# Summing the exponentials of both key halves on TensorE in a conditioned transformer block

## The chip, the cores and the metric

The kernel runs on one core of one Trainium2 chip. The metric is the time of one execution on the device in microseconds; lower is better. Before the change it is 2498.34 us, the median of three runs (2495.81 to 2498.56).

## The reference

One pre-norm transformer block in fp32 on `x` of 4 x 1024 x 512, with norms whose gain and bias come from a conditioning vector. There are 16 heads of 32 channels and 2048 hidden channels.

```python
g = t @ gw.T + gb; b = t @ bw.T + bb
norm(x) = g * x * rsqrt(mean(x * x) + EPS) + b
attn = (q . k) / sqrt(32); p = softmax(attn); o = (p . v)
x1  = x  + o @ Wo.T
x2  = x1 + (silu(n @ gate_w.T) * (n @ hid_w.T)) @ out_w.T    # n = norm2(x1)
out = x + x2
```

What matters here is the softmax: every query needs the sum of its exponentials over all 1024 keys, for each head.

## The kernel before, in words

Activations lie channels first: partitions are channels, columns are tokens. Attention works on units `j`: one batch element and half a block of 512 queries (so 256 queries, `HQ`), and one group of four heads (`HG`). There are 64 units. A unit takes its 1024 keys in four steps `r` (`UN` = 4) of two key tiles of 128 keys each. A step's scores are one tile `raw[r]` of 128 partitions (keys) by 2 x 4 x 256 columns: key tile `k` in 0..1, head, query.

A step passes through these operations, named as in the code:

- `scores` (TensorE, L301) computes the scores, `keep` (ScalarE, L308) copies them out of PSUM, and `running_max` (VectorE, L313 and L316) keeps the largest per head and query over the keys that share a partition.
- After the four steps, `max_T` (TensorE, L322), `parts` (VectorE, L328 to L333), `parts_T` (L338, L340) and `spread` (L348, L349) turn the maximum into a tile `shift` that every key's partition can add.
- `shifted` (VectorE, L354) adds it, `exponential` (ScalarE, L357) takes the exponential in place, and `weighted` (TensorE, L367) multiplies with the values into `av`.
- `accumulate` (L381) adds the step's exponentials onto those of the unit's first step. This is a DMA that adds, issued by GpSimd, over all 2 x 4 x 256 columns. So after four steps the tile `acc[j]` holds, for each partition, key tile `k`, head and query, the sum over four steps.
- `fold_sum` (VectorE, L389) then adds the half `k` = 1 onto the half `k` = 0, 128 x 1024 numbers.
- `sums` (TensorE, L399) sums over the partitions: one matmul with a 128 x 32 tile of ones for each head, so that the head's 32 output partitions all hold the sum. `sums_out` (ScalarE, L404), `inverse` (L407) and `normalize` (L416) follow.

The order on TensorE, VectorE, ScalarE and GpSimd is written out by hand in one loop over `g`, one step of scores in each turn; each engine works through its own list in that order. `kind` is `g % 4`. Behind the scores of step `g` come `shifted` and `exponential` of step `g - 5` and `weighted` of step `g - 6`. `fold_sum` of a unit stands at the end of the turn of kind 3, and `sums` of the same unit in the next turn, of kind 0, ahead of `max_T` of a later unit. The last DMA of `accumulate` was issued two turns before `fold_sum`.

The rest of the work fills the same turns. In the first 500 us these are the projections (`project_kq`, `project_v`) and norms of later batch elements; from about 540 us it is the feed-forward part, one hidden tile of 128 channels in two turns. Its seven products for a tile (a Strassen-like scheme) go by `pair_15`, `pair_26`, `pair_7`, `pair_3` and `pair_4` into the PSUM tiles `pa` and `pb`; around them stand `take_5` (L511) and `copy_156` (L530) on ScalarE, `add_15` (L515) and `sub_5` (L537) on VectorE, `gate` (L552) and `hidden` (L555). `contract` (tile `pc`) multiplies four hidden tiles with the output weights, and `take_contract` (L568) adds that onto the result. `add_15` stands on VectorE just ahead of `fold_sum`, `hidden` just behind it. In some turns `token_sums` (L482 to L488), `norm_squares` (L132 to L138), `norm_root` (tiles `pma` and `pmf`) and `project_out` (tile `po`) come in too. After 2213 us no attention unit is left, only the last output projection, its norm and the feed-forward part.

`sum`, `pc`, `pa`, `pt`, `sp`, `pma` and others share two PSUM banks (tag `w`, two buffers): a matmul into a new tile waits until the tile two before it has been read out.

Of the kernel before, what the change touches and what calls it, by code (L numbers as in the profile page):

```python
# [13 lines left out]
ALU = mybir.AluOpType  # L14
# [10 lines left out]
def tile_cond_transformer_block(  # L25
# [13 lines left out]
    nc = tc.nc  # L39
# [7 lines left out]
    DH = D // N_HEADS  # L47
    HG = P // DH
# [22 lines left out]
    ones_sum = const.tile([P, DH], F32, tag="ones_sum", name="ones_sum")  # L71
# [39 lines left out]
    raw, rmax, shift, mT, av, acc, avs, oT = {}, {}, {}, {}, {}, {}, {}, {}  # L111
# [180 lines left out]
    def scores(r: int):  # L292

        j, u = divmod(r, UN)
        m, qh = divmod(j, NB // HQ)
        keys, queries = kq[m, 0, u], kq[m, 1, qh]
        sc = ps_sc.tile([P, HG, 2, HQ], F32, tag="sc", name=f"sc{r}")
        for k in range(2):
            for i in range(HG):
                rows = slice(i * DH, (i + 1) * DH)  # L300
                nc.tensor.matmul(  # L301
                    sc[:, i, k, :], keys[rows, k * P : (k + 1) * P], queries[rows, :], start=True, stop=True
                )
        state["sc", r] = sc
# [30 lines left out]
    def parts_T(j: int):  # L335
        pt = ps.tile([P, HQ // P, P], BF16, tag="w", name=f"pt{j}")
        for qt in range(HQ // P):
            nc.tensor.transpose(pt[:, qt, :], split[j % 2][:, qt, :], ident_bf)  # L338
        mT[j] = sb.tile([NP, HQ], BF16, tag="mT", name=f"mT{j}", bufs=2)
        nc.scalar.copy(mT[j], pt[:NP, :, :].rearrange("p a b -> p (a b)"))  # L340

    def spread(j: int, k: int):

        if k == 0:
            shift[j] = sb.tile([P, HG, HQ], F32, tag="shift", name=f"shift{j}")
        pp = ps.tile([P, 2, HQ], F32, tag="w", name=f"sp{j}_{k}")
        for i in range(2):
            nc.tensor.matmul(pp[:, i, :], select[:, k + i, :], mT[j], start=True, stop=True)  # L348
        nc.scalar.copy(shift[j][:, k : k + 2, :], pp)  # L349
# [6 lines left out]
    def exponential(r: int):  # L356
        nc.scalar.activation(raw[r], raw[r], AF.Exp)  # L357
# [26 lines left out]
                accum_op=ALU.add,  # L384
            )

    def fold_sum(j: int):
        t = acc[j]
        nc.vector.tensor_tensor(t[:, 0, :, :], t[:, 0, :, :], t[:, 1, :, :], ALU.add)  # L389

    def take_av(j: int):
        avs[j] = sb.tile([P, HQ], F32, tag="avs", name=f"avs{j}", bufs=2)
        nc.scalar.copy(avs[j], av.pop(j))

    def sums(j: int):
        total = ps.tile([P, HQ], F32, tag="w", name=f"sum{j}")
        a = acc.pop(j)
        for i in range(HG):
            nc.tensor.matmul(total[i * DH : (i + 1) * DH, :], ones_sum, a[:, 0, i, :], start=True, stop=True)  # L399
        state["sum", j] = total  # L400

    def sums_out(j: int):
# [3 lines left out]
    def inverse(j: int):  # L406
        nc.vector.reciprocal(state["total", j], state["total", j])  # L407
# [280 lines left out]
    with tc.manual_schedule(  # L688
# [69 lines left out]
        while g < END:  # L758
            kind = g % UN
            r_x, r_v = g - UN - 1, g - UN - 2  # L760
            x_on, v_on = 0 <= r_x < NR, 0 <= r_v < NR
            j_m = g // UN - 1
            m_on = 0 <= j_m < NR // UN
            j_s = g // UN - 2
            s_on = 0 <= j_s < NR // UN
            j_n = g // UN - 3
            n_on = 0 <= j_n < NR // UN
            ffn = g >= FS
            p = (g - FS) // 2
            even = g % 2 == 0  # L770
            columns[0] = DH

            if kind == 1 and m_on:
                parts_T(j_m)
            if g < NR:
                scores(g)
            if kind == 1 and m_on:
                spread(j_m, 0)

            if kind == 2 and n_on and j_n < direct:  # L780
                inverse(j_n)
                if j_n % (BS // UN):
                    normalize(j_n)
            if kind == 1 and n_on and j_n % (BS // UN) == 1:
                normalize(j_n - 1)
            if x_on and kind != 1:
                shifted(r_x)
            if late is not None:
                late()
                late = None  # L790
            for fn, a in pinned.pop(g, []):
                fn(*a)
            if v_on:
                weighted(r_v)
                accumulate(r_v)
            if kind == 1 and m_on:
                spread(j_m, 2)
                mT.pop(j_m)
                shifted(r_x, slice(0, HG // 2))
                shifted(r_x, slice(HG // 2, HG))  # L800
            if g < NR:
                keep(g)
            if kind == 1 and s_on:
                take_av(j_s)
            due = bool(first) and first[0][0] <= g
            if not ffn:
                if x_on:
                    exponential(r_x)
                evict = chain(g, FG)
                if kind == 0:  # L810
                    take_sums(j_n)
                if g < NR:
                    running_max(g, 0)
                    running_max(g, 1)
                if kind == 0 and m_on:
                    columns[0] = P
                    max_T(j_m)
                    parts(j_m)
                if evict is not None:
                    evict()  # L820
                for fn, a in halfway.pop(g, []):
                    fn(*a)
                if g == FS - 1:
                    columns[0] = DH
                    pair_15(0)
                    take_5(0)
                    add_15(0)
                elif even:
                    late = chain(g, FG)
                if kind == 3 and s_on:  # L830
                    fold_sum(j_s)
                if g in (FS - 4, FS - 2):
                    load_f((g - FS + 4) // 2)
            elif even:
                load_f(p + 2)
                pair_26(p)
                copy_156(p)
                if kind == 0:
                    take_sums(j_n)
                if x_on:  # L840
                    exponential(r_x)
                if kind == 0 and m_on:
                    max_T(j_m)
                    parts(j_m)
                one, two, evict = filler(p)
                one()
                two()
                if g < NR:
                    running_max(g, 0)
                    running_max(g, 1)  # L850
                if evict is not None:
                    evict()
                pair_7(p)
                sub_5(p)
                for fn, a in halfway.pop(g, []):
                    fn(*a)
            else:
                extra = due or len(queue) > FG
                evict = None
                if kind == 3 and extra:  # L860
                    evict = chain(g)
                pair_3(p)
                if kind == 3:
                    gate_tanh(p)
                if x_on:
                    exponential(r_x)
                pair_15(p + 1)
                take_5(p + 1)
                for fn, a in amid.pop(g, []):
                    fn(*a)  # L870
                if kind == 1:
                    gate_tanh(p)
                    if extra:
                        spare_bank[0] = True
                        evict = chain(g)
                if g < NR:
                    running_max(g, 0)
                if kind == 3 and evict is not None:
                    evict()
                if kind == 3:  # L880
                    gate(p)
                if g < NR:
                    running_max(g, 1)
                add_15(p + 1)
                if kind == 1:
                    gate(p)
                    if evict is not None:
                        evict()
                if kind == 3 and s_on:
                    fold_sum(j_s)  # L890
                pair_4(p)
                hidden(p)
                if due:
                    chain(g)()
                for fn, a in halfway.pop(g, []):
                    fn(*a)
            columns[0] = DH
            for fn, a in ended.pop(g, []):
                fn(*a)
            if g == FS + 2 * FG - 2:  # L900
                load_ow(0)
            g += 1
# [90 lines left out]
```

## Time and profile before

| | |
|---|---|
| median of three runs | 2498.34 us |
| the profiled execution, its own time | 2495.65 us |
| its span, first to last instruction | 2493.8 us |
| TensorE: matmuls busy / weight loads busy | 2392.5 us / 1125.5 us |
| VectorE busy | 1941.8 us |
| ScalarE busy | 1406.4 us |
| mean granted TensorE clock | 0.998 |
| `fold_sum` (L389): 64 instructions | 77.7 us on VectorE |
| `sums` (L399): 512 matmul records | 39.4 us on TensorE |

A row of instruction groups names line, engine, operation, the tile written and the tiles read, shapes and count; then busy time in us, the mean of one in ns, and the engine's idle time just before them with what ended it. A row of a timeline gives the start, the duration, the engine, the line and the count of instructions merged in it, and in brackets the idle time before it and what ended that. Matmuls overlap in their pipeline, and the end of each is modelled: the distance from one start to the next says more than the durations. TensorE shows two records for each fp32 matmul.

### The profile page before, as it was taken

The numbers are of one execution on the slowest core, as the hardware profiler recorded it, in microseconds if no ns is written. First come the engines' busy times: TensorE is split into PE (matmuls) and PEld (weight loads), VectorE is DVE, ScalarE is ACT, GpSimd is POOL, SyncE is SP. The second block draws the span as 40 slices with busy tenths as digits, with TensorE's granted clock in tenths as the row PEclk, the third lists the DMA queues.
The fourth block names the chain that finished last, engine by engine and source line by source line (L and its number), as shares of the span: only waits on it lengthen the run. The fifth ranks groups of instructions, "written<-read, shape, count | busy, mean of one in ns | idle before, by whom it ended". The sixth has DMA issues, their size and how long they took to land. (4 is left out here: it accounts for less than half of the span.)

```text
span 2493.8 us, 71084 instructions
## 1 busy us (share of the span) xinstructions
PE 2392.5 (96%) x31749; PEld 1125.5 (45%) x31749; DVE 1941.8 (78%) x2180; ACT 1406.4 (56%) x1488; POOL 172.4 (7%) x207
## 2 busy tenths in 40 slices
PE   8999999999999999999999999999999999999999
PEld 3333333345444444444444444444444444444444
DVE  2688888878979997999789988998899979843332
ACT  3677667766656665666566656665666656522111
POOL 0000000000000000000000000000000000000000
PEclk9999999999999999999999999999999999999999
DMA  6698999888878898888878888889788978863442
GB/s 213 175 290 242 239 250 235 221 209 230 209 174 205 210 229 200 194 207 225 203 186 202 234 191 199 207 214 221 180 204 195 240 183 202 195 177 112 141 131 73
DMA packets 185982, 501.69 MB, mean 201 GB/s; under 512 B 21319, under 2 KB 78663, under 8 KB 158286
## 3 DMA queue, kind: packets, MB, share of 16 engines
q0 software_dynamic: 28656, 208.68, 42.7%
q1 hardware_dynamic: 154704, 288.42, 35.3%
q8 instruction: 250, 4.10, 0.6%
q10 hardware_dynamic: 2318, 0.05, 0.1%
q14 instruction: 54, 0.44, 0.1%
HBM read 246.44 MB, written 41.97 MB: 116 GB/s over the span
## 5 line engine op out<-in xcount | busy, mean ns | idle before, releaser
L354 DVE TENSOR_TENSOR raw<-raw,shift 128x2048 f32<-128x2048 f32 (+1 forms) x320 | 594.1, 1857 | 101.7 <-ACT shift L349 98.2
L357 ACT ACTIVATE raw<-raw 128x2048 f32<-128x2048 f32 x256 | 490.9, 1918 | 321.2 <-DVE raw L354 321.0
L308 ACT COPY raw<-sc 128x2048 f32<-128x2048 f32 x256 | 478.8, 1870 | 86.0 <-PE sc L301 44.0
L313 DVE TENSOR_TENSOR rmax<-rmax,raw 128x1024 f32<-128x1024 f32 x384 | 469.1, 1222 | 58.1 <-ACT raw L308 53.2
L106 PE MATMUL pc<-h,ow 128*32 128x512 f32 x4096 | 467.9, 593 | 2.3 <-ACT total L404 1.1
L367 PE MATMUL av<-raw,v 128*32 128x256 f32 x4096 | 274.1, 385 | 61.5 <-ACT raw L357 55.1
L381 POOL DMA_DIRECT2D raw<-raw x192 | 165.3, 861 | 2009.0 <-ACT raw L357 945.4
L301 PE MATMUL sc<-q,k 32*128 32x256 f32 x4096 | 293.3, 400 | 1.8 <-ACT raw L308 1.8
L106 PE MATMUL pa<-x,fa 128*32 128x256 f32 x4096 | 269.1, 380 | 8.1 <-DVE pa L515 8.0
L106 PE MATMUL pa<-sums,fw 128*32 128x256 f32 x4096 | 267.9, 379 | 0.0
L106 PEld LDWEIGHTS pc<-h,ow 128*32 128x32 f32 x4096 | 127.6, 110 | 246.5 <-issue 221.6
L301 PEld LDWEIGHTS sc<-q,k 32*128 32x128 f32 x4096 | 184.9, 184 | 117.8 <-issue 79.4
L106 PE MATMUL pkq<-y,wkq 128*32 128x512 f32 (+1 forms) x1664 | 231.6, 594 | 4.2 <-ACT y L187 4.1
L367 PEld LDWEIGHTS av<-raw,v 128*32 128x32 f32 x4096 | 106.9, 109 | 188.3 <-ACT raw L357 109.8
L106 PEld LDWEIGHTS pa<-x,fa 128*32 128x32 f32 x4096 | 127.5, 109 | 122.8 <-DVE pa L515 28.8
L106 PEld LDWEIGHTS pa<-sums,fw 128*32 128x32 f32 x4096 | 133.1, 110 | 87.9
L530 ACT COPY pb<-pa 128x256 f32<-128x256 f32 x128 | 46.3, 362 | 179.5 <-PE pa L106 174.9
L547 ACT ACTIVATE t<-pa 128x512 f32<-128x512 f32 x128 | 78.0, 609 | 119.7 <-PE pa L106 119.6
L106 PE MATMUL pa<-x,fw 128*32 128x256 f32 x2048 | 135.2, 381 | 0.0
L106 PE MATMUL pb<-x,fw 128*32 128x256 f32 x2048 | 134.0, 379 | 1.2 <-ACT pb L530 1.2
L106 PE MATMUL pb<-sums,fa 128*32 128x256 f32 x2048 | 134.0, 379 | 0.0
L106 PEld LDWEIGHTS pkq<-y,wkq 128*32 128x32 f32 (+1 forms) x1664 | 73.2, 116 | 131.5 <-issue 119.4
(104 smaller groups left out, 2166.0 us busy)
## 6 DMA issues: line engine op xcount, KB each, us to landing
raw<-raw POOLq DMA_DIRECT2D x192, 1024.0 KB, 9.2
fw<-sw SPq DMA_DIRECT2D x128, 512.0 KB, 5.8
fa<-in_gh_w SPq DMA_DIRECT2D x128, 384.0 KB, 7.8
ow<-in_out_w SPq DMA_DIRECT2D x128, 256.0 KB, 3.4
wkq<-in_kq_w SPq DMA_DIRECT2D x32, 512.0 KB, 9.1
v<-vs SPq DMA_DIRECT2D x128, 128.0 KB, 6.0
k<-kqs SPq DMA_DIRECT2D x124, 128.0 KB, 7.7
kqs<-st SPq DMA_DIRECT2D x61, 256.0 KB, 6.3
```

The costliest lines, as they stand in the source:

```text
L106: nc.tensor.matmul(dst[k : k + n, :], w[:, k : k + n], moving, start=start, stop=stop, skip_group_check=seeded)
L301: nc.tensor.matmul(sc[:, i, k, :], keys[rows, k * P : (k + 1) * P], queries[rows, :], start=True, stop=True)
L308: nc.scalar.copy(raw[r].rearrange("p k h q -> p h k q"), state.pop(("sc", r)))
L313: nc.vector.tensor_tensor(rmax[j], rmax[j], raw[r][:, k, :, :], ALU.max)
L354: nc.vector.tensor_tensor(t, t, s.unsqueeze(1).to_broadcast(list(t.shape)), ALU.add)
L357: nc.scalar.activation(raw[r], raw[r], AF.Exp)
L367: nc.tensor.matmul(av[j][i * DH : (i + 1) * DH, :], v[m, u][:, k, i * DH : (i + 1) * DH], raw[r][:, k, i, :], start=(kt == 0), stop=(kt == ...
L381: nc.gpsimd.dma_start(out=acc[j].rearrange("p k h q -> p (k h q)"), in_=raw[r].rearrange("p k h q -> p (k h q)"), accum_op=ALU.add,)
L530: nc.scalar.copy(bank_b[p][:, RIGHT], bank_a[p][:, RIGHT])
L547: nc.scalar.activation(state["t", p], bank_a[p], AF.Tanh, scale=0.5)
```

## The change

`fold_sum` is removed with both its calls. `sums` now reads both halves of `acc[j]`: four matmuls on half 0 that start the sum and four on half 1 that add to it in PSUM.

```diff
-    def fold_sum(j: int):
-        t = acc[j]
-        nc.vector.tensor_tensor(t[:, 0, :, :], t[:, 0, :, :], t[:, 1, :, :], ALU.add)
-
     def sums(j: int):
         total = ps.tile([P, HQ], F32, tag="w", name=f"sum{j}")
         a = acc.pop(j)
-        for i in range(HG):
-            nc.tensor.matmul(total[i * DH : (i + 1) * DH, :], ones_sum, a[:, 0, i, :], start=True, stop=True)
+        for k in range(2):
+            for i in range(HG):
+                nc.tensor.matmul(
+                    total[i * DH : (i + 1) * DH, :], ones_sum, a[:, k, i, :], start=k == 0, stop=k == 1
+                )
         state["sum", j] = total
...
-                if kind == 3 and s_on:
-                    fold_sum(j_s)
                 if g in (FS - 4, FS - 2):
                     load_f((g - FS + 4) // 2)
...
-                if kind == 3 and s_on:
-                    fold_sum(j_s)
                 pair_4(p)
                 hidden(p)
```

## The prediction

> **What bounds the kernel now.** I read the page's busy times first, then the groups kept apart by shape, then the idle times before each line's instructions, then the timeline of one unit in each stage.
>
> ```profile
> PE 2392.5 (96%) x31749; PEld 1125.5 (45%) x31749; DVE 1941.8 (78%) x2180; ACT 1406.4 (56%) x1488; POOL 172.4 (7%) x207
> ```
>
> ```profile
> L389 DVE TENSOR_TENSOR raw<-raw 128x1024 f32<-128x1024 f32 x64 | 77.7, 1214 | 1.1 <-DMA raw<-raw 1.1
> ...
> L399 PE MATMUL sum<-raw,ones_sum 128*32 128x256 f32 x512 | 39.4, 379 | 0.4 <-PE pa L106 0.4
> ```
>
> TensorE (PE) is busy 96% of the span, but its durations overlap, so I took distances from start to start. Sixteen records of 256 columns (`pa`, for example) step 0.863 us wherever nothing waits; with no attention left, after 2300 us, the same step repeats unbroken. Taking for each kind of block of matmuls its tenth percentile as the undisturbed step, everything above it sums to 177 us over the span. TensorE works for some 93% of the time; a matmul more is paid for unless it falls into one of those waits. VectorE (DVE) has 22% idle time, so what it saves counts only where TensorE waits for what is queued behind the fold. A feed-forward turn shows who waits:
>
> ```profile
> 1273.61 0.42 DVE L515 TENSOR_TENSOR pa<-pa,p 128x256 f32<-128x256 f32 x1
> 1273.95 1.21 DVE L389 TENSOR_TENSOR raw<-raw 128x1024 f32<-128x1024 f32 x1
> ...
> 1274.09 1.07 PE L106 MATMUL pa<-x,fa 128*32 128x256 f32 x16 [0.19 <-DVE pa L515]
> ...
> 1274.98 1.05 PE L106 MATMUL pa<-sums,fw 128*32 128x256 f32 x16
> ...
> 1275.68 2.28 DVE L354 TENSOR_TENSOR raw<-raw,shift 128x2048 f32<-128x2048 f32 x1
> 1275.85 0.61 PE L399 MATMUL sum<-raw,ones_sum 128*32 128x256 f32 x8
> ...
> 1276.39 1.09 PE L322 MATMUL mt<-ident,rmax 128*128 128x128 f32 x8
> ...
> 1277.88 1.22 DVE L328 TENSOR_REDUCE top<-mt 128x8 f32<-128x1024 f32 x1
> 1277.99 1.91 ACT L357 ACTIVATE raw<-raw 128x2048 f32<-128x2048 f32 x1 [1.09 <-DVE raw L354]
> ...
> 1283.34 1.07 PE L367 MATMUL av<-raw,v 128*32 128x256 f32 x16
> ...
> 1284.07 2.54 DVE L354 TENSOR_TENSOR raw<-raw,shift 128x1024 f32<-128x1024 f32 x2 [1.51 <-ACT shift L349]
> ```
>
> TensorE does wait for VectorE here, but for L515, which stands ahead of the fold. `sum` follows `pa` at the `pa` step (1274.98 to 1275.85), with no wait for the fold. What stands behind the fold is L354 for the next exponential (L357), which ends at 1279.90, while its reader `av` is reached at 1283.34: 3.4 us of slack. Then VectorE stands idle 1.51 us for `shift`, which comes from TensorE. There the 1.21 us are lost: VectorE only waits longer.
>
> **The change, part by part.** *Added:* 64 units times four matmuls, two records each, so 512 records of 128x32 weights and 256 columns. By the step of `pa`, one costs 0.863/16 = 0.0539 us, so a unit pays 8 x 0.0539 = 0.431 us and all units 27.6 us. Bounds: nothing where TensorE waits anyway; 39.4 us by the busy time of the existing 512. I take the step: the form is the same, in the same sequence.
>
> The whole of today's `sum` block steps 0.546 us, which is 8 x 0.0539 plus 0.115; sixteen should step 0.98. The same 0.114 shows between `pb` (0.977 in place of 0.863) and a scores block with another shape of array. [...]
>
> *Removed:* 64 x 1.214 = 77.7 us of VectorE. Unit by unit, what comes behind the fold:
>
> - 52 units look like the one above, or like it in the early stage: VectorE next idles for TensorE or ScalarE, nothing on TensorE comes earlier, and the sum's 0.431 us shifts everything behind it. 52 x 0.431 = +22.4 us.
> - Six units (fold at 810, 1074, 1338, 1601, 1865, 2129 us) have L486 of `token_sums` behind the fold as well. There VectorE is late: `pt` waits for L568 and comes about 0.45 us later than in other units. Without the fold L568 is ready when `pc` is, so that wait goes, while the sum adds 0.431 us: about -0.05 us each, -0.3.
> - Five units in the first 420 us have `norm_root` behind the sum, and there the chain passes through the fold:
>
> ```profile
> 205.45 1.22 DVE L389 TENSOR_TENSOR raw<-raw 128x1024 f32<-128x1024 f32 x1
> ...
> 206.59 1.48 DVE L138 TENSOR_TENSOR tota<-tota,sqa 128x512 f32<-128x512 f32 x2
> ...
> 207.98 2.29 DVE L354 TENSOR_TENSOR raw<-raw,shift 128x2048 f32<-128x2048 f32 x1
> ...
> 210.30 1.91 ACT L357 ACTIVATE raw<-raw 128x2048 f32<-128x2048 f32 x1 [1.94 <-DVE raw L354]
> ...
> 212.12 0.35 ACT L404 COPY total<-sum 128x256 f32<-128x256 f32 x1
> ...
> 212.53 1.12 PE L106 MATMUL pma<-tota,ones_mean 128*128 128x512 f32 x2 [1.43 <-ACT total L404]
> ```
>
> TensorE waits for the copy of the sum (L404), queued on ScalarE behind an exponential whose L354 stands behind the fold. Without the fold L138 starts earlier, until it must wait for its squares instead: these end at 206.61, so the second L138 ends at 207.30 and not 208.07, about 0.7 us gained. The unit at 138.6 gains 1.15 by the same reckoning, those at 205.5, 343.3 and 410.7 gain 0.7, that at 272.8 nothing (L138 already waits for its square). The wait also hides the sum's 0.431. Together -3.25 us.
> - The last unit: its fold sits 1.11 us until the last accumulating DMA lands (2210.7), and delays `hidden`, `sum`, L404 and `pc` (2213.37). Without it `sum` can follow `pa` at 2211.45, ends near 2212.52, and L404 lets `pc` go at about 2213.0: -0.35 us.
>
> *Moved waits:* `sum` already waited for the accumulating DMA; it now does so without the fold in between. Queued behind it on TensorE are `max_T` and all that follows. In 63 units the landing is 5.9 us or more ahead of `sum`, in the last 1.4 us, so it costs nothing; were it later, TensorE would stop in full. The first L354 of most units now carries the wait for an earlier accumulating DMA that the fold had carried; the `keep` into that buffer had to wait for it anyway. ScalarE's, GpSimd's and SP's lists stay as they were.
>
> Sum: 22.4 - 0.3 - 3.25 - 0.35 = +18.5 us. On the profiled execution (2495.65, of which 1.85 lies outside the span) that gives 2514.2; it lay 2.7 us below the median of the runs, so on the median 2498.34 + 18.5 = 2516.8 us. A difference under 0.2%, 5 us, can hardly be told from none.
>
> [...]
>
> **The rivals.** *Full price:* the waits in the 12 special units come back later (the exponential that `av` waits for 20 us after a fold in the early stage), and nothing is given back: +27.6, 2525.9 us. For it: those later waits exist, 1.5 us each. Against: VectorE idles 4.7 us for TensorE in between (unit at 205.5), so they move along.
>
> *VectorE on the path:* TensorE waits some 85 us in all between scores and `av`, for exponentials behind L354. If VectorE's earlier start after the fold reached those waits, a unit would gain 1.214 - 0.431 = 0.783 us; it breaks even with 0.431/1.214 = 36% of units, 23 of 64, and all 64 give -50.1: 2448 us. Against: those waits come in turns of kind 0 and 3, and in every feed-forward unit VectorE has idled at kind 1 in between.
>
> *The sum absorbed:* the same waits swallow the 0.431 us because VectorE, not TensorE, sets the pace from kind 1 to kind 0. Then only the 12 units count, with -3.9 us: 2494 us; half of it 2505. Against: VectorE's run starts with `shift`, which TensorE makes after the sum and so equally late.
>
> *Dearer matmuls:* 39.4 us by busy time, or DMAs that land behind `sum`: about 2538 us.
>
> **How the numbers follow.** Chances: forecast 0.66 (its own range 2508 to 2522), full price 0.16, VectorE on the path 0.07, absorbed 0.07, dearer 0.04. The range 2508 to 2527 holds the first two: its low end lets twenty more units absorb their 0.431 us, its high end is the full price plus 1 us of spread between runs; 0.18 is left out. Faster 0.07; same 0.07, which is the absorbed case; slower 0.86.
>
> **What would show it.** Right: the `sum` block with 16 records steps 0.98 us to `mt`; VectorE's idle time before L354 of kind 1 grows by more than 1 us; an ordinary feed-forward unit, 30.5 us from fold to fold now, takes 30.9; `pma` after `sum` comes earlier relative to it in the four named units; `pt` of the L486 units loses its wait. Wrong: units of 30.5 us or less (VectorE was on the path, or the sum is absorbed), a `sum` step above 1.1 us, or `sum` waiting for a DMA.

## The result, and the profile after

The changed kernel takes 2516.57 us (median of four runs, 2516.03 to 2517.84), against 2497.4 us before (four runs, 2495.81 to 2498.56): the ratio is 1.0078, with a 95% interval of 1.006 to 1.0095. It is slower by 19.2 us by the medians. The profiled execution took 2516.40 us, 20.75 more than that of before; its span is 2514.6 us.

The page's busy times after, to be read against the same line of before: TensorE has 512 records and 28.5 us more, VectorE 64 instructions and 67.4 us less (78% to 75% of the span). That is less than the 77.7 us of `fold_sum`, because each fold overlapped the instructions on both sides of it by some 0.08 us (77.7 - 67.4 us over 64 folds and two sides).

```profile
PE 2421.0 (96%) x32261; PEld 1142.2 (45%) x32261; DVE 1874.4 (75%) x2116; ACT 1402.6 (56%) x1488; POOL 172.4 (7%) x207
```

From the groups kept apart by shape, one line of before, the row of L328:

```profile
L328 DVE TENSOR_REDUCE top<-mt 128x8 f32<-128x1024 f32 x64 | 77.8, 1216 | 11.4 <-PE mt L322 11.4
```

After the change, the sum's matmuls and the two VectorE lines in which I looked for the time that the fold set free (busy us, mean ns, idle us before them and what ended it):

```profile
L354 DVE TENSOR_TENSOR raw<-raw,shift 128x1024 f32<-128x1024 f32 x128 | 156.6, 1225 | 95.5 <-ACT shift L349 91.9
...
L328 DVE TENSOR_REDUCE top<-mt 128x8 f32<-128x1024 f32 x64 | 78.3, 1223 | 60.6 <-PE mt L322 60.6
...
L396 PE MATMUL sum<-raw,ones_sum 128*32 128x256 f32 x1024 | 67.0, 379 | 0.0
```

The 1024 records of the sum never waited. VectorE's saving turned into waiting: its idle time before L328, which needs the transposes of `max_T` from TensorE, went from 11.4 to 60.6 us. Most of the rest appears before L316 (40.2 to 56.6 us) and before `take_contract` (53.2 to 69.1 us).

The timeline of the feed-forward unit that was shown before. `sums` is L396 now, and the lines behind it count one lower; the `av` in the first line is the one ahead of the fold's old place (before, it started at 1272.83):

```profile
1283.12 1.07 PE L367 MATMUL av<-raw,v 128*32 128x256 f32 x16
...
1284.24 0.69 DVE L554 TENSOR_TENSOR h<-pb,h 128x512 f32<-128x512 f32 x1
...
1284.84 2.29 DVE L354 TENSOR_TENSOR raw<-raw,shift 128x2048 f32<-128x2048 f32 x1
...
1286.14 1.05 PE L396 MATMUL sum<-raw,ones_sum 128*32 128x256 f32 x16
...
1287.12 1.09 PE L322 MATMUL mt<-ident,rmax 128*128 128x128 f32 x8
...
1288.25 1.23 DVE L328 TENSOR_REDUCE top<-mt 128x8 f32<-128x1024 f32 x1 [1.12 <-PE mt L322]
```

`sum` to `mt` is now 0.98 us (1286.14 to 1287.12), where it was 0.54. `hidden` (L554) and L354 come 1.1 us earlier relative to that `av` than before, and VectorE then stands idle for 1.12 us before L328 until TensorE is through.

For all that follows I measured in each trace the distance from the start of one unit's `sum` on TensorE to the next one's (from the `max_T` of the same turn to the next one where the sum itself is moved), and took the difference to the same distance before. This ledger, worked out from the starts in the traces, shows where a kernel pays. For the changed kernel:

| units (0 to 63, by their sum) | change for each |
|---|---|
| ordinary units, about 50 | +0.43 |
| the six with L486 (20, 28, 36, 44, 52, 60) | -0.01 to -0.03 |
| with `norm_root`: unit 0; units 2, 6, 8 | -1.13; -0.46 |
| with `norm_root`: unit 4 | +1.70, where 0 was forecast; the granted TensorE clock was 0.50 in 3.4 us of it (see the end) |
| units 9 and 14; unit 62, ahead of the last sum | +0.27 and +0.36; -0.20 |

### The profile page after: what moved, and what is told of

It is laid out like the page before. It is cut to its first block, busy times and chain, and to the rows that moved or that the text cites. A ratio compares the mean times of both kernels' runs of the same rounds, so it can differ in the third digit from the quotient of the medians.

```text
span 2514.6 us, 72115 instructions
## 1 busy us (share of the span) xinstructions
PE 2421.0 (96%) x32261; PEld 1142.2 (45%) x32261; DVE 1874.4 (75%) x2116; ACT 1402.6 (56%) x1488; POOL 172.4 (7%) x207
## 5 line engine op out<-in xcount | busy, mean ns | idle before, releaser
L354 DVE TENSOR_TENSOR raw<-raw,shift 128x2048 f32<-128x2048 f32 (+1 forms) x320 | 594.7, 1859 | 95.5 <-ACT shift L349 91.9
L313 DVE TENSOR_TENSOR rmax<-rmax,raw 128x1024 f32<-128x1024 f32 x384 | 469.4, 1222 | 58.2 <-ACT raw L308 53.3
L567 DVE SCALAR_TENSOR_TENSOR res<-pc,res 128x512 f32<-128x512 f32 x128 | 88.2, 689 | 69.1 <-PE pc L106 69.1
L340 ACT COPY mT<-pt 12x256 bf16<-12x256 bf16 x64 | 23.1, 361 | 200.9 <-PE pt L338 200.9
```

The source lines that it names most:

```text
L313: nc.vector.tensor_tensor(rmax[j], rmax[j], raw[r][:, k, :, :], ALU.max)
L354: nc.vector.tensor_tensor(t, t, s.unsqueeze(1).to_broadcast(list(t.shape)), ALU.add)
L567: nc.vector.scalar_tensor_tensor(r, pp, 0.5, r, ALU.mult, ALU.add)
```

## The experiments

Every experiment ran 4 to 11 times beside the kernel before on the same chip; the times given are medians.

**The matmuls alone: the fold stays, the sum's matmuls are doubled.**

```diff
-        for i in range(HG):
-            nc.tensor.matmul(total[i * DH : (i + 1) * DH, :], ones_sum, a[:, 0, i, :], start=True, stop=True)
+        for _ in range(2):
+            for i in range(HG):
+                nc.tensor.matmul(total[i * DH : (i + 1) * DH, :], ones_sum, a[:, 0, i, :], start=True, stop=True)
```

> The fold stays on VectorE, and the four matmuls of the sum are issued twice (both times on the folded half, each starting afresh, so the value is the same). TensorE gets the whole added work of the change, VectorE keeps its own. Theory (TensorE sets the pace; each unit pays 0.431 us unless TensorE waits there anyway): 53 of 64 units pay, the five units with norm_root and the six with L486 behind the fold hide it, so +22.8 us; unit distance 30.5 becomes 30.9 us. Rival (the matmuls are dearer than their step, and the removed fold paid part of it back in ordinary units): well over the changed kernel's +19 us, +36 to +39 by the busy time of the existing sums. Rival (the sum is absorbed): within 5 us.

Measured: 2518.7 against 2496.78 us, +21.9, ratio 1.0086 (1.0073 to 1.01). In the ledger ordinary units pay +0.43 or +0.44; the L486 units and units 0, 2 and 6 of those with `norm_root` pay 0.00 to 0.01. The other two with `norm_root`, 4 and 8, are longer (+1.36 and +1.69): the granted TensorE clock was 0.98 in the 100 us around each (300 to 400 and 400 to 500 us), where before it was 1.00. One early unit (14) is 0.75 shorter, which stays unexplained. So the price of the matmuls is what their step says, with VectorE's work untouched, and the changed kernel's loss is this price.

**The fold alone: no fold, four matmuls.**

```diff
-                if kind == 3 and s_on:
-                    fold_sum(j_s)
```

Both calls go, against the kernel before; `sums` stays as it was.

> No fold and only the four matmuls on half 0: the second half of the summed exponentials is left out of the sum. VectorE loses its 77.7 us and TensorE gets nothing more. Theory: only the units whose fold has TensorE waiting behind it gain: the five with norm_root together 2.5 us (as the changed kernel's trace shows), six with L486 0.45 us each, the last 0.8 us: -6 us, ordinary units unchanged at 30.5 us. Rival (VectorE's time is on the path in many units): -20 to -50 us, ordinary units shorter.

Measured: 2489.84 against 2496.78 us, -6.9, ratio 0.9973 (0.9962 to 0.9983). The ledger: ordinary units 0.00 to 0.01; the L486 units -0.45 or -0.46 each; unit 0 -1.13, three others -0.46 or -0.47; the last -0.62. So 77.7 us of VectorE's work are worth 7 us. They are worth it in the units where the profile showed TensorE waiting for something queued behind the fold, and next to nothing elsewhere (the largest is -0.17, in unit 9).

**More work in the same place: the fold twice.**

```diff
         nc.vector.tensor_tensor(t[:, 0, :, :], t[:, 0, :, :], t[:, 1, :, :], ALU.add)
+        nc.vector.tensor_tensor(t[:, 0, :, :], t[:, 0, :, :], t[:, 0, :, :], ALU.max)
```

> Kernel before with a second VectorE instruction of the fold's size right behind it (a maximum of the folded half with itself, which changes nothing). It asks whether VectorE's 22% idle time is room for more in the same place. Theory: no. In some 46 feed-forward units the fold just fits: L568 starts 0.06 us after the wait for pc would let it, pt waits for L568, so 1.21 us more there come out at about 1.15 us a unit; with up to 5 us from the norm_root units, +50 us. Rival (idle share is room): within 5 us.

Measured: 2560.12 against 2496.78 us, +63.3, ratio 1.025 (1.0236 to 1.0264). Most ordinary feed-forward units pay 1.11 us for 1.21 us of work, L486 units 1.25; two in every eight (16 and 17, 24 and 25, and so on) pay 0.43 and 0.68. The timeline of this kernel, around the transposes of one such unit:

```profile
1316.20 1.22 DVE L316 TENSOR_TENSOR rmax<-raw 128x1024 f32<-128x1024 f32 x1
...
1317.34 0.68 DVE L569 SCALAR_TENSOR_TENSOR res<-pc,res 128x512 f32<-128x512 f32 x1
...
1318.07 0.27 PE L338 MATMUL pt<-ident_bf,split 128*128 128x128 bf16 x2 [0.35 <-DVE res L569]
```

`take_contract` (here L569) follows L316 without a gap, though `pc` ends at 1316.86 (start 1313.22, 3.64 us), and `pt` waits for it. The place is asymmetric in these units: taking the fold away gains nothing, adding as much again costs nearly its whole length. VectorE's idle share of 22% was no room there. Most of the 13 us over the expectation lie in the first 480 us, where I had counted 5 us: the ledger shows 16.6 us there. Part is the TensorE clock: it was granted at 0.97 between 200 and 300 us and at 0.95 between 300 and 400 us, where the trace of before has 1.00 (see the end). Over the whole span the mean was 0.994 against 0.998, which by my estimate is worth some 10 us at most (0.004 of 2558 us); what the rest is stays open.

**The addition on GpSimd.**

```diff
-        nc.vector.tensor_tensor(t[:, 0, :, :], t[:, 0, :, :], t[:, 1, :, :], ALU.add)
+        nc.gpsimd.tensor_tensor(t[:, 0, :, :], t[:, 0, :, :], t[:, 1, :, :], ALU.add)
...
+            if kind == 3 and s_on:
+                fold_sum(j_s)
             if v_on:
                 weighted(r_v)
```

The two old calls at the end of the turn go.

> The fold's addition moves to GpSimd, at the start of the same turn, ahead of that turn's accumulating DMA; four matmuls on the folded half as before. Nothing of GpSimd's addition is in a trace yet, so its time is open. Theory: VectorE and TensorE then do what they do in the run without a fold, -6 us, if GpSimd's addition ends before sum (it can start 7 to 9 us ahead of it) and does not slow VectorE's instructions that run beside it. Rival (GpSimd's addition is late, or holds up the accumulating DMAs behind it, or slows VectorE beside it): slower than before, seen as sum waiting for GpSimd or as longer L313/L354.

Measured: 2586.09 against 2496.78 us, +89.3, ratio 1.0357 (1.0343 to 1.0371). The rival held, in its last form: VectorE is slowed. From the timeline:

```profile
1102.22 4.54 DVE L313 TENSOR_TENSOR rmax<-rmax,raw 128x1024 f32<-128x1024 f32 x2
...
1103.28 2.40 POOL L389 TENSOR_TENSOR raw<-raw 128x1024 f32<-128x1024 f32 x1 [9.25 <-DMA raw<-raw]
```

Two `running_max` (L313) that take 2.47 us when alone take 4.54 us beside GpSimd's 2.40 us. GpSimd's addition (2.56 us in the median, against 1.21 on VectorE) was done in time in all but one unit, but it took nearly its own length from VectorE. Many ordinary units pay about 2.1 us. Over the span L313 is busy 60 us longer than before (469.1 to 529.1) and L354 on 2048 columns 19 us (437.6 to 456.6). The mean granted TensorE clock was 0.991 against 0.998, which by my estimate adds at most some 18 us (0.007 of 2582 us).

**Each unit by what it pays: fold in 53 units, both halves on TensorE in eleven.**

```diff
+    BOTH = {0, 2, 6, 8, 20, 28, 36, 44, 52, 60, 63}
...
+        if j in BOTH:
+            return
...
+        halves = 2 if j in BOTH else 1
```

> The fold on VectorE and four matmuls in 53 units, no fold and eight matmuls in eleven: four with norm_root behind the sum (units 0, 2, 6, 8), six with L486 (20, 28, 36, 44, 52, 60) and the last (63). Theory: in ordinary units nothing changes; in the eleven the added matmuls are hidden, or paid for by the wait that goes: -1.13, three times -0.46, six times -0.02, -0.4, so -3 us against the kernel before, near the edge of what can be told. Rival (what the special units gain is given back later): 0. Rival (the fold's absence is what slows the changed kernel): slower.

Measured: 2493.7 against 2497.66 us, -4.0, ratio 0.9984 (0.9975 to 0.9993). Ordinary units stay at 0.00 (but for 9 and 14, at -0.17 and +0.31). So the gains of the special units are kept and not given back.

**The sum's matmuls in TensorE's waits.** Two kernels put the eight matmuls (no fold) where TensorE waits for VectorE's chain, into the free half of the bank of `av`. In the first the place is kind 3:

```diff
+        beside = j + 1 in av
+        if beside:
+            total = av[j + 1][:, HQ:]
+        else:
+            total = ps.tile([P, HQ], F32, tag="w", name=f"sum{j}")
...
+                    start=k == 0 and not beside,
...
+            if kind == 3 and s_on and j_s + 1 in av:
+                sums(j_s)
             if v_on:
                 weighted(r_v)
```

> The changed kernel, but the eight matmuls of a unit's sum stand one turn earlier, ahead of weighted of kind 3, where TensorE waits for an exponential; the sum goes into the free right half of the PSUM bank of av (started by av's own first matmul), not into a tile of tag w. Theory: VectorE sets when that wait ends, so the eight matmuls (0.86 us) fill waits of 0.5 to 1.6 us there and of 0.4 us behind, and the turn of kind 0 loses its sum block of 0.55 us: up to -0.5 us in each of some 40 ordinary units on top of the -6 us of the run without a fold, -10 to -25 us. It is paid down by units whose last accumulating DMA has not landed yet: in the profile of before, five units land 2.5 to 4.1 us after that place. Rival (TensorE sets the pace everywhere, waits are no room): +19 us as in the changed kernel, or more.

Measured: 2503.6 against 2497.66 us, +5.9, ratio 1.0026 (1.0017 to 1.0035). The total missed the expectation; the ledger says why. Most ordinary feed-forward units gained 0.34 to 0.43, those with L486 up to 0.80; six with `project_out` behind the sum (17, 25, 33, 41, 49, 57) paid 0.43, and five units (23, 31, 39, 47, 55, the very ones whose DMA had landed too late for that place in the profile of before) cost 4.0 to 6.7 us each. One of them:

```profile
891.56 1.93 PE L400 MATMUL av<-raw,ones_sum 128*32 128x256 f32 x16 [5.12 <-DMA raw<-raw]
```

TensorE stood 5.12 us for the accumulating DMA, with nothing of its list done in between, and then ran at half clock (0.50 from 892.0 to 895.4 us). The second kernel places the same matmuls at kind 0:

```diff
-            if kind == 3 and s_on and j_s + 1 in av:
-                sums(j_s)
+            if kind == 0 and n_on and j_n + 1 in av:
+                sums(j_n)
```

> As the run before it, but the eight matmuls stand ahead of weighted of kind 0, some 5.5 us later, where every DMA has landed; the waits there are smaller (0.1 us for the exponential, 0.37 us for L515). Theory: 0.86 us go in, 0.47 are hidden, 0.55 leave the later place: -0.1 us in an ordinary unit, -6 to -12 us in all. Rival (waits are no room): +19 us.

Measured: 2485.31 against 2497.66 us, -12.3, ratio 0.995 (0.9938 to 0.9963). Ordinary feed-forward units come out at +0.03 and +0.04, close to free; those with `project_out` pay 0.43; the rest of the gain lies in the special and the early units. The place and the PSUM bank moved together here, and no run moves one alone; but in the changed kernel the sum's matmuls never waited at the old place, so a wait of theirs for a tile of tag `w` is not what was saved.

**Placed by unit.**

```diff
+    LATE = {15, 19, 23, 31, 39, 47, 55}
+    FOLDED = {17, 25, 33, 41, 49, 57}
...
+            if kind == 3 and s_on and j_s + 1 in av and j_s not in LATE | FOLDED:
+                sums(j_s)
+            if kind == 0 and n_on and j_n in LATE:
+                sums(j_n)
```

> No fold and eight matmuls ahead of weighted of kind 3 in most units, as in the run with the sum in that wait; the seven units whose last DMA landed after or close to that place in the traces (15, 19, 23, 31, 39, 47, 55) have their sum ahead of weighted of kind 0; the six with project_out behind, which paid 0.43 us in both placements (17, 25, 33, 41, 49, 57), keep the fold on VectorE, with four matmuls at the old place. Theory (waits that VectorE sets are room; a late DMA and the clock drops behind it were what the earlier placement cost): six late units give back 26 us, six folded ones 2.6 us, so about -20 to -26 us against the kernel before. Rival (the saved time makes other DMAs late, since they are paced by themselves): new units of +4 us, and a total above -10 us.

Measured: 2476.93 against 2497.29 us, -20.4, ratio 0.9921 (0.9908 to 0.9935). It is faster than the kernel before and than the changed one. The late units are back at +0.04, the folded ones at 0.00. The rival has a part: units 32 and 40 now wait 1.06 and 1.85 us for their accumulating DMA and pay +0.80 and +1.58. Before, these landed 1.8 and 2.1 us ahead of that place. With such waits the gain is at the lower end.

## Why the prediction was right, point by point

- **Forecast and measure.** 2516.8 us was forecast, 2516.57 measured. That the two agree within 0.3 us is partly luck: the forecast starts from 2498.34, and with a fourth run the median of before is 2497.4, so that +18.5 was forecast and +19.2 measured. On the profiled execution 2514.2 was forecast and 2516.40 came, 2.2 us more; the steps below account for that.
- **The price of a matmul.** The `sum` block stepped 0.98 us as forecast, units paid 0.43, and the doubled matmuls under an untouched fold cost 21.9 us. The bound of 39.4 us by busy time would have been wrong: busy rose by 27.6 us (39.4 to 67.0).
- **One surplus.** That a block of sixteen records pays the surplus of 0.115 us once, as the block of eight did, was my estimate from the two rows of before. The trace after shows it: the block steps 0.98 us, sixteen times 0.0539 and one surplus of 0.11. The new matmuls added none of their own, which by my estimate would have been 64 x 0.114 = 7.3 us.
- **VectorE's saving worth nothing in ordinary units.** Shown by the run without a fold (0.00 to 0.01 there). I put the lost time in the wrong place, though: VectorE's idle time before L354 of kind 1 did not grow (101.7 to 95.5 us). VectorE already stands before L328 of kind 0. The conclusion was the same, since both wait for TensorE.
- **The six L486 units.** -0.05 each forecast, -0.01 to -0.03 measured; without the added matmuls -0.45, the size read from the wait of `pt`.
- **The units with `norm_root`.** -1.15, three times -0.7 and 0 forecast; -1.13 and three times -0.46 measured. For unit 4 the 0 holds in the runs without the fold and in the mixed one (0.01 and 0.00); in the changed kernel the clock hides it. The step that was mis-sized: I let the second L138 start when its square ends, but the first one must wait for its own square and the two then run one after the other. In the trace after, L138 waits 0.58 us and the pair ends 0.45 us earlier, not 0.7. That is 0.7 us in all.

```profile
204.44 1.15 ACT L132 ACTIVATE sqa<-y 128x512 f32<-128x512 f32 x2
...
205.11 1.49 DVE L138 TENSOR_TENSOR tota<-tota,sqa 128x512 f32<-128x512 f32 x2 [0.58 <-ACT sqa L132]
```

- **The last unit.** `sum` follows `pa` with no wait, as forecast. From the `pa` ahead of the sum to `pc` the unit is 0.37 us shorter than before, against 0.35 forecast.
- **The landing.** The last accumulating DMA lands 4.5 and 4.6 us ahead of `sum` in units 47 and 39 of the trace before, not 5.9 or more as read. The conclusion stands: no record of the sum waited.
- **What was not forecast.** Between the sums of units 4 and 5 TensorE ran at half clock for 3.4 us; that distance grew by 1.70, of which the block of `pkq` took 1.48. With the 0.7 us this makes 2.4; small terms, the largest a first sum that came 0.31 us earlier, leave 2.2.
- **The rivals.** Full price falls, because the special units' gains stayed (-4.0 us in the mixed run). VectorE on the path and the absorbed sum are refuted for ordinary units by the two runs that change one side alone. The waits that were to pay for them do exist: put into them, the added matmuls are nearly free (+0.03 us in ordinary units, at kind 0). The change left the sum behind them, in the part of the turn that TensorE paces.
- **Weight loads.** Their busy share stayed at 45% (1125.5 us before, 1142.2 after), and still a matmul record more cost its full step of 0.0539 us, 0.43 for the eight added to a unit.

## What to carry to other kernels

Price work for a saturated engine by the start-to-start step of its neighbours, not by busy time or shares (here a unit's four added matmuls cost the 0.43 us of the step, where busy time gave 39.4/64 = 0.62), and then ask for each repetition whether that engine waits at that spot. For work taken from another engine, follow what is queued behind it to the first place where that engine idles: where the saturated engine had not waited by then, the saving was worth nothing here (0.00 to 0.01 us a unit), and 1.21 us more of work already cost 1.11. Before moving work between engines, look for the waits of the saturated one and try to put the work there, with the landing of its DMA checked unit by unit.

## What the runs showed of the hardware that I had not expected

TensorE's granted clock dropped to half in the middle of the span, for 3.41 us just behind a wait of 2.45 us. Here are two stretches of the changed kernel's trace and then two of the trace before (PEclk is the granted clock):

```profile
308.00:311.40 3.40, 0.95 (x23) 0.45 (x19) 3.37 (x4) 2.68 (x3) 0.47 (x1) 0.99 1.01 299
311.40:314.90 3.50, 3.50 (x24) 1.06 (x20) 1.89 (x1) 3.50 (x4) 0.39 (x1) 0.52 0.75 210
```

```profile
307.20:310.70 3.50, 2.07 (x28) 0.80 (x20) 3.50 (x3) 1.79 (x2) 0.00 (x0) 1.00 1.02 221
310.70:314.10 3.40, 2.39 (x32) 1.07 (x36) 3.37 (x4) 3.40 (x5) 0.86 (x1) 1.00 0.94 280
```

The columns after the stretch are its length, then PE, PEld, DVE, ACT and POOL busy with their counts, PEclk, the DMA share and GB/s. TensorE stood 2.45 us for an exponential (308.2 to 310.7), and the clock was 0.52 in the 3.5 us after it. Before, the same wait was 2.44 us and brought no drop; in the run with the sum at kind 3 the wait of 5.12 us did (0.50 over 3.4 us).

What goes with this drop can be read from the clock records of the two traces; no run tried it apart. All changes of the clock that the changed kernel's trace records from 14.38 us on (at 14.38, 21.21, 311.34, 314.75 and 2512.94 us) lie whole multiples of 3.413 us apart: 2, 85, 1 and 644. So do the three of before (13.70, 20.52 and 2491.77 us: 2 and 724). I cut each trace between 60 and 2400 us into steps of that length, counted from those changes, 1369 steps in all, and summed TensorE's matmul records (whose ends are modelled) in each. The step of the changed kernel from 307.9 to 311.3 us has the least, 0.96 us, and the clock fell behind it. The others have 1.73 us or more, and it fell behind none of them. In the changed kernel the wait lies within that one step; before, it was split over two (the last two rows, with 2.07 and 2.39 us). One drop in two traces is no rule yet.

A wait in TensorE's list thus cost more than its length here. By my estimate 3.41 us at half clock are worth 1.7 us at most (half of 3.41), and the distance with the drop in it grew by 1.70 us; that favours filling such a wait.
